# The last 128 query columns of a head in one tile: a rope with half-tile products and a rotation of three twin matmuls

## The chip, the cores and the metric

The kernel runs on one core of a Trainium2 chip. The metric is the device time of one execution in microseconds (us). Three runs of the kernel before took 2216.96, 2220.8 and 2221.03 us, a median of 2220.8 us. The profile is of one further execution.

The engines are named as in the profile: PE (TensorE) multiplies matrices into PSUM, the accumulator memory; PEld is its weight load; DVE (VectorE) and ACT (ScalarE) work elementwise from PSUM or SBUF, the on-chip memory; POOL (GpSimd) works on SBUF; SP issues transfers.

## The reference

The reference is a two-layer block on x of shape (4, 512, 512) in float32. Layer 0 is a top-k sparse adjacency and a ternary feed-forward. Layer 1 is a cross attention with 16 heads and rotary embedding, and a second ternary feed-forward. The change lies in the query side of the layer-1 attention:

```
q_hk  = (hidden_q @ Wq.T).reshape(B, S, 16, 128)
q_big = einsum('bshk,hkq->bshq', q_hk, w_kc_q)        # 384 columns per head
q_big = q_big * cos + rotate_half(q_big) * sin
q_r   = einsum('bshq,hqr->bhsr', q_big, W_qr)         # 64 columns per head
scores = einsum('bhsr,bhlr->bhsl', q_r, k_r)
```

`rotate_half` pairs column i with column i + 192 (the first half gets the second with a minus sign). So each of the 384 columns has one rotation partner, 192 away.

## The kernel before, in words

Tensors stand transposed: query columns lie on partitions and the 512 positions of one batch along the free dimension. 128 partitions hold 128 of the 384 columns. The code names four chunks (`_query_chunks`): a is columns 0-127, a1 is 192-319 (the partners of a), c is 128-191 and c1 is 320-383 (the partners of c). c and c1 have 64 columns each.

Heads are taken in pairs, an even one e and an odd one o; 4 batches times 8 pairs make 32 pairs. `Pair.head(i)` (line 677) computes q_hk of head i. `Pair.rope(i)` (lines 685-710) makes the columns and rotates them:

- `rope(0)` takes a and a1 of head e, `rope(1)` takes a and a1 of head o: two full 128 x 128 matmuls each (line 693), one for a and one for a1.
- `rope(2)` takes the rest of both heads. Its first tile holds c of e on partitions 0-63 and c of o on 64-127, the second holds c1 in the same way. Each tile comes from two matmuls with 64 output columns each, called twins here (`halves`, lines 661-665).

In every rope a tile and its partner tile have the same partitions. So each rotated tile takes two products on DVE over all 128 partitions, ro = tile x cos (line 707) and rs = partner x sin (line 708), and one sum on POOL (line 709).

`Pair.rotated` (lines 712-731) sums q_r of both heads in one PSUM tile pr, with e in partitions 0-63 and o in 64-127. For a and for a1 it issues one twin pair each (e and o side by side). For the tiles of `rope(2)`, which mix e and o along the contraction, it uses two full matmuls (line 726) with a block-diagonal weight: 64 x 64 of e, 64 x 64 of o, zeros elsewhere. ACT then copies pr to SBUF as qr (line 731).

`attention` walks over the 32 pairs. While the current pair does its scores (lines 744 and 747), softmax (752-758), transposes (766), values (774) and output (786), the next pair's `head` and `rope` are mixed in: `rope(2)` in the fourth of four steps, `rotated` after the values. The first pair's head, ropes and rotation stand ahead of the loop.

A generator of background work runs beside it, metered by a table of costs: for batches 1 to 3 the layer-0 adjacency (`adjacency`, whose top-k search alternates a MAX8 at line 403 with a MATCH_REPLACE8 at line 405, 20 rounds for each of four tiles) and the layer-0 feed-forward (`feed0`), later the weights and rows of the second feed-forward (`feed1`). The framework that builds the kernel fixes one order of instructions per engine from the program order and its own estimate of when inputs are ready. So each engine works through a list, and a change of one part shifts background instructions elsewhere in the lists.

PSUM tiles of attention come from a pool of four buffers (`mm_ps`), which pb, pss, pc, pr and po share. The weights of a pair (`query_weights`) are loaded on SP's queue one pair ahead; wr holds the W_qr rows of both heads.

Of the kernel before, what the change touches and what calls it, by code (L numbers as in the profile page):

```python
# [9 lines left out]
F32 = mybir.dt.float32  # L10
BF = mybir.dt.bfloat16
AF = mybir.ActivationFunctionType
ALU = mybir.AluOpType
AX = mybir.AxisListType

P = 128
B, S, D = 4, 512, 512
# [5 lines left out]
NH = 16  # L23
# [10 lines left out]
def flamingo_kernel(  # L34
# [9 lines left out]
    nc = tc.nc  # L44

    const = ctx.enter_context(tc.tile_pool(name="const", bufs=1))
# [5 lines left out]
    hp = ctx.enter_context(tc.tile_pool(name="heads", bufs=2))  # L52
# [5 lines left out]
    def mm_ps(name):  # L58
        return ps.tile([P, 512], F32, tag="mm", name=name)
# [57 lines left out]
    wqk = const.tile([P, 2, DC], F32, tag="wqk", name="wqk")  # L117
    nc.scalar.dma_start(wqk[:, 0, :], wq0T)
    nc.scalar.dma_start(wqk[:, 1, :], wk0T)
    cos_q = const.tile([P, 4, S], F32, tag="cosq", name="cos_q")  # L120
    sin_q = const.tile([P, 4, S], F32, tag="sinq", name="sin_q")

    gx_raw = const.tile([P, 5], F32, tag="graw", name="gx_raw")
    nc.scalar.dma_start(gx_raw[:, 0:2], g_x.partition_broadcast(P))
# [513 lines left out]
    def query_weights(b, g):  # L638

        u = f"{b}_{g}"  # L640
        wqs = []
        for i in range(2):
            wq = hp.tile([P, NC, P], F32, tag="wq", name=f"wq_{u}_{i}")
            nc.sync.dma_start(wq, wqh[2 * g + i])
            wqs.append(wq)
        wc = hp.tile([P, 6 * P], F32, tag="wc", name=f"wc_{u}", bufs=1)
        nc.sync.dma_start(wc, wkcq[g])
        wr = hp.tile([P, 4 * P], F32, tag="wr", name=f"wr_{u}", bufs=1)
        nc.sync.dma_start(wr, wqr[g])
        return wqs, wc, wr  # L650

# [9 lines left out]
    def halves(o, lhs, rhs, **flags):  # L661

        nc.tensor.matmul(o[64:, :], lhs[1], rhs[1], skip_group_check=True, **flags)  # L663
        with tc.high_priority():
            nc.tensor.matmul(o[:64, :], lhs[0], rhs[0], skip_group_check=True, **flags)

    class Pair:
# [17 lines left out]
        def rope(self, i):  # L685


            both = []
            for o in range(2):
                pb = mm_ps(f"pb_{self.u}_{i}_{o}")  # L690
                if i < 2:
                    at = (2 * i + o) * P
                    nc.tensor.matmul(  # L693
                        pb, self.wc[:, at : at + P], self.qhs[i], start=True, stop=True
                    )
                else:
                    at = (4 + o) * P
                    halves(
                        pb, (self.wc[:, at : at + 64], self.wc[:, at + 64 : at + P]), self.qhs,
                        start=True, stop=True,  # L700
                    )
                both.append(pb)
            for o in range(2):
                t = 2 * (i // 2) + o
                ro = wp.tile([P, S], F32, tag="ro", name=f"ro_{self.u}_{i}_{o}", bufs=7)
                rs = wp.tile([P, S], F32, tag="rs", name=f"rs_{self.u}_{i}_{o}", bufs=3)
                nc.vector.tensor_tensor(ro, both[o], cos_q[:, t, :], ALU.mult)  # L707
                nc.vector.tensor_tensor(rs, both[1 - o], sin_q[:, t, :], ALU.mult)  # L708
                nc.gpsimd.tensor_tensor(ro, ro, rs, ALU.add)  # L709
                self.ros.append(ro)  # L710

        def rotated(self):

            wr, ros, u = self.wr, self.ros, self.u
            self.kr = wp.tile([P, S], F32, tag="kr", name=f"kr_{u}", bufs=1)
            nc.sync.dma_start(self.kr, kr_d[self.b, self.g])
            pr = mm_ps(f"pr_{u}")
            for o in range(2):
                halves(
                    pr,  # L720
                    (wr[:, 64 * o : 64 * o + 64], wr[:, P + 64 * o : P + 64 * o + 64]),
                    (ros[o], ros[2 + o]),
                    start=(o == 0), stop=False,
                )
            for o in range(2):
                nc.tensor.matmul(  # L726
                    pr, wr[:, (2 + o) * P : (3 + o) * P], ros[4 + o],
                    start=False, stop=(o == 1), skip_group_check=True,
                )
            self.qr = wp.tile([P, S], F32, tag="qr", name=f"qr_{u}", bufs=1)  # L730
            nc.scalar.copy(self.qr, pr)
            self.pT = [
                wp.tile([P, NT, S], F32, tag="pT", name=f"pT_{u}_{i}") for i in range(2)
            ]
# [58 lines left out]
    def begin(b, g):  # L793
        p = Pair(b, g)
        p.wqs, p.wc, p.wr = query_weights(b, g)
        return p
# [100 lines left out]
    for _ in attention(first):  # L897
        done += 1
        while job < len(jobs):
            gen, cost, until = jobs[job]  # L900
            start = jobs[job - 1][2] if job else 0
# [23 lines left out]
def _hadamard(n):  # L925
    import numpy as np

    h = np.ones((1, 1), np.float32)
    while h.shape[0] < n:
        h = np.block([[h, h], [h, -h]])  # L930
    return np.ascontiguousarray(h, dtype=np.float32)


def _rope(length, dim):
    import numpy as np

    inv = np.float32(1.0) / np.power(
        np.float32(10000.0), np.arange(0, dim, 2, dtype=np.float32) / np.float32(dim)
    )
    f = np.arange(length, dtype=np.float32)[:, None] * inv.astype(np.float32)[None, :]  # L940
    return (
        np.repeat(np.sin(f), 2, axis=-1).astype(np.float32),
        np.repeat(np.cos(f), 2, axis=-1).astype(np.float32),
    )


def _constants():
    import numpy as np

    sin, cos = _rope(S, DQ)  # L950
    half = DQ // 2
    sign = np.where(np.arange(DQ) < half, -1.0, 1.0).astype(np.float32)
    sin = sin * sign
    a, a1, c, c1 = _query_chunks()
    order = np.concatenate([a, a1, c, c, c1, c1])
    q = lambda t: np.ascontiguousarray(t.T[order].reshape(4, P, S).transpose(1, 0, 2))
    cosq, sinq = q(cos), q(sin)
    sin, cos = _rope(S, DC)
    sin = sin * np.where(np.arange(DC) < DC // 2, -1.0, 1.0).astype(np.float32)
    k = lambda t: np.ascontiguousarray(t.reshape(NT, P, DC).transpose(1, 0, 2))  # L960
    return {"had": _hadamard(P), "cosq": cosq, "sinq": sinq, "cosk": k(cos), "sink": k(sin)}


def _query_chunks():

    import numpy as np

    half = DQ // 2
    a, c = np.arange(P), np.arange(P, half)
    return a, a + half, c, c + half  # L970


def _pair_columns(w):

    import numpy as np

    a, a1, c, c1 = _query_chunks()
    e, o = w[0::2], w[1::2]
    return np.concatenate(
        [e[:, :, a], e[:, :, a1], o[:, :, a], o[:, :, a1],  # L980
         e[:, :, c], o[:, :, c], e[:, :, c1], o[:, :, c1]], axis=2
    )


def _pair_rows(w):


    import numpy as np

    a, a1, c, c1 = _query_chunks()  # L990
    e, o = w[0::2], w[1::2]
    z = np.zeros((NH // 2, 64, 64), w.dtype)
    block = lambda r: np.concatenate(
        [np.concatenate([e[:, r], z], axis=2), np.concatenate([z, o[:, r]], axis=2)], axis=1
    )
    return np.concatenate([e[:, a], e[:, a1], o[:, a], o[:, a1], block(c), block(c1)], axis=2)


_OUT = ((B, S, D), "float32")
# [46 lines left out]
```

## Time and profile before

| what | value |
|---|---|
| median of 3 runs | 2220.8 us |
| the profiled execution, its own time | 2219.97 us |
| its span, first to last instruction | 2218.2 us |
| mean granted PE clock | 0.932 |
| PE / DVE / ACT / POOL busy | 1932.9 / 1582.2 / 1225.4 / 350.8 us |
| matmul records, DVE instructions | 7402, 3124 |
| line 726 (block-diagonal matmuls of q_r) | 128 records, 63.8 us |
| lines 663 and 665 in pb (twins of `rope(2)`) | 128 records each, 71.0 us each |
| lines 707 and 708 (rope products on DVE) | 192 each, 130.9 and 131.1 us |
| line 709 (rope sums on POOL) | 192, 256.6 us |

How to read it: a float32 matmul leaves two records. Ends of matmuls are modelled and overlap the next start, so the distance from start to start is the time that a matmul takes of PE. The group lines give, after the bar, busy us, mean ns of one instruction, and the idle time of the engine just before them with what ended it. All engines work at once: idle time counts only on the engine that sets the pace.

### The profile page before, as it was taken

To read this page: it belongs to the slowest core of one execution; us is meant where nothing else is said; L and a number is where in the kernel's file an instruction comes from. 1 tells how busy PE (TensorE), PEld (TensorE's weight loads), DVE (VectorE), ACT (ScalarE), POOL (GpSimd) and SP (SyncE) were. 2 spreads that over 40 slices of the span, in tenths; PEclk is the share of its full clock that TensorE was granted. 3 is DMA by queue.
4 is the path that set the end of the run, shared out by engine and by line. 5 is a ranking of instruction groups with operands and counts; after the bars stand their busy time and mean duration, and the time that the engine had idled before them with its cause. 6 is when DMAs were issued, how large, how long until landed. Compare 5 with 4: busy or idle time off the path is not lost. (4 is left out here: it accounts for less than half of the span.)

```text
span 2218.2 us, 21879 instructions
## 1 busy us (share of the span) xinstructions
PE 1932.9 (87%) x7402; PEld 913.9 (41%) x7402; DVE 1582.2 (71%) x3124; ACT 1225.4 (55%) x1997; POOL 350.8 (16%) x332
## 2 busy tenths in 40 slices
PE   1359789999989989899989888999979999999978
PEld 0125434344444334445443334444434444444433
DVE  7977699976675999665569997566635645756665
ACT  6826444344655543456455543555699565557534
POOL 3032021122110111211111112201211210111000
PEclk6579899999999999899999998999989999999889
DMA  7442011110010211110102111011457101111000
GB/s 275 154 156 94 34 43 38 48 41 27 31 36 24 77 44 36 36 41 24 36 27 83 41 48 36 25 36 32 151 204 244 50 28 53 57 36 34 14 15 20
DMA packets 62176, 140.30 MB, mean 63 GB/s; under 512 B 7152, under 2 KB 10608, under 8 KB 58736
## 3 DMA queue, kind: packets, MB, share of 16 engines
q1 hardware_dynamic: 56592, 122.44, 17.0%
q0 software_dynamic: 4320, 14.16, 1.7%
q10 hardware_dynamic: 1152, 2.30, 0.3%
q8 instruction: 59, 0.97, 0.2%
q14 instruction: 53, 0.43, 0.1%
HBM read 118.95 MB, written 19.92 MB: 63 GB/s over the span
## 5 line engine op out<-in xcount | busy, mean ns | idle before, releaser
L709 POOL TENSOR_TENSOR ro<-ro,rs 128x512 f32<-128x512 f32 x192 | 256.6, 1341 | 1464.0 <-DVE rs L708 1330.7
L755 ACT ACTIVATE pp<-pss,nm 128x512 f32<-128x512 f32 x256 | 174.7, 685 | 247.8 <-DVE nm L752 246.7
L774 PE MATMUL pc<-pT,kv 128*128 128x512 f32 x512 | 259.7, 644 | 8.7 <-ACT pT L767 8.6
L677 PE MATMUL pqh<-hT,wq 128*128 128x512 f32 x512 | 240.2, 608 | 0.7 <-ACT hT L635 0.7
L786 PE MATMUL po<-om,cxo 128*128 128x512 f32 x512 | 229.9, 593 | 0.0
L752 DVE TENSOR_REDUCE nm<-pss 128x1 f32<-128x512 f32 x256 | 169.5, 682 | 65.1 <-PE pss L747 63.8
L403 DVE MAX8 m<-work 128x8 f32<-128x512 f32 x304 | 210.5, 692 | 5.4
L766 PE MATMUL ppt<-ident,pp 128*128 128x128 f32 x1024 | 160.4, 294 | 47.6 <-ACT pp L758 35.5
L405 DVE MATCH_REPLACE8 work<-m,work 128x512 f32<-128x512 f32 x288 | 195.1, 677 | 0.0
L758 ACT ACTIVATE pp<-pp,rsm 128x512 f32<-128x512 f32 x256 | 178.8, 721 | 27.8 <-DVE rsm L757 25.6
L791 DVE SCALAR_TENSOR_TENSOR x<-po,gt,x 128x512 f32<-128x512 f32 x128 | 95.7, 748 | 135.1 <-PE po L786 134.9
L767 ACT COPY pT<-ppt 128x512 f32<-128x512 f32 x256 | 142.7, 588 | 85.8 <-PE ppt L766 84.7
L766 PEld LDWEIGHTS ppt<-ident,pp 128*128 128x128 f32 x1024 | 126.9, 151 | 132.8 <-ACT pp L758 54.7
L707 DVE TENSOR_TENSOR ro<-pb,cos_q 128x512 f32<-128x512 f32 x192 | 130.9, 682 | 34.8 <-PE pb L693 33.9
L744 PE MATMUL pss<-kr,qr 64*128 64x512 f32 x256 | 145.5, 649 | 8.3 <-ACT pp L755 7.7
L747 PE MATMUL pss<-kr,qr 64*128 64x512 f32 x256 | 146.3, 652 | 1.8 <-DVE ro L707 1.3
L677 PEld LDWEIGHTS pqh<-hT,wq 128*128 128x128 f32 x512 | 93.0, 191 | 127.7 <-issue 93.1
L774 PEld LDWEIGHTS pc<-pT,kv 128*128 128x128 f32 x512 | 99.0, 207 | 103.6 <-issue 87.0
L786 PEld LDWEIGHTS po<-om,cxo 128*128 128x128 f32 x512 | 95.8, 190 | 110.0 <-issue 108.1
L693 PE MATMUL pb<-qh,wc 128*128 128x512 f32 x256 | 123.4, 601 | 15.6 <-DVE ro L707 14.9
L708 DVE TENSOR_TENSOR rs<-pb,sin_q 128x512 f32<-128x512 f32 x192 | 131.1, 683 | 7.7 <-PE pb L693 3.5
L779 ACT COPY cxo<-pc 128x512 f32<-128x512 f32 x64 | 37.4, 585 | 120.8 <-PE pc L774 120.7
(256 smaller groups left out, 3285.6 us busy)
## 6 DMA issues: line engine op xcount, KB each, us to landing
wq<-in_wqh SPq DMA_DIRECT2D x64, 256.0 KB, 2.6
om<-omd SPq DMA_DIRECT2D x64, 256.0 KB, 2.7
wc<-in_wkcq SPq DMA_DIRECT2D x32, 384.0 KB, 3.0
wr<-in_wqr SPq DMA_DIRECT2D x32, 256.0 KB, 2.6
krd<-krs POOLq DMA_DIRECT2D x32, 256.0 KB, 2.3
kr<-krd SPq DMA_DIRECT2D x32, 256.0 KB, 2.6
sa_w1v<-in_gvT SPq DMA_DIRECT2D x8, 1024.0 KB, 5.0
sb_w1v<-in_gvT SPq DMA_DIRECT2D x8, 1024.0 KB, 6.5
```

The lines of the kernel that those rows point to most:

```text
L403: nc.vector.max(m8, cur)
L405: nc.vector.match_replace(work, m8, cur, GONE)
L677: nc.tensor.matmul(pq, self.wqs[i][:, c, :], hT[self.b][:, c, :], start=(c == 0), stop=(c == NC - 1),)
L709: nc.gpsimd.tensor_tensor(ro, ro, rs, ALU.add)
L744: nc.tensor.matmul(*args, start=True, stop=True)
L747: nc.tensor.matmul(*args, start=True, stop=True)
L752: nc.vector.tensor_reduce(nm, pss[i], AX.X, ALU.max, negate=True)
L755: nc.scalar.activation(pp, pss[i], AF.Exp, bias=nm, accum_out=sm)
L758: nc.scalar.activation(pp, pp, AF.Copy, scale=rs)
L766: nc.tensor.transpose(pt[:, l, :], pp[:, l * P : (l + 1) * P], ident)
L774: nc.tensor.matmul(pc, kv[self.b][:, l, :], self.pT[i][:, l, :], start=(l == 0), stop=(l == NT - 1),)
L786: nc.tensor.matmul(po, self.cxo[i][:, j * P : (j + 1) * P], self.oms[i], start=(i == 0), stop=(i == 1),)
```

## The change

The 64 + 64 remaining columns of one head now share a tile: `rope(2)` puts c and c1 of head e into its first tile, and c and c1 of head o into its second. The rotation partner of a column then lies in the same tile, 64 partitions away.

- The two tiles come from one full 128 x 128 matmul each, like those of the other ropes. `halves` is no longer used there.
- The cos and sin tables have three tiles instead of four; the third serves both heads.
- For the tiles of `rope(2)` the product with sin is done in two halves: partitions 64-127 of the tile go to partitions 0-63 of rs, and 0-63 to 64-127. The products with cos and the sums stay whole.
- `rotated` issues three twin pairs, since now every rotated tile belongs to one head. The block-diagonal weight is gone, and wr shrinks from four to three blocks of 128 columns.
- On the host, weights and tables are laid out to match.

```diff
-    cos_q = const.tile([P, 4, S], F32, tag="cosq", name="cos_q")
-    sin_q = const.tile([P, 4, S], F32, tag="sinq", name="sin_q")
+    cos_q = const.tile([P, 3, S], F32, tag="cosq", name="cos_q")
+    sin_q = const.tile([P, 3, S], F32, tag="sinq", name="sin_q")
...
-        wr = hp.tile([P, 4 * P], F32, tag="wr", name=f"wr_{u}", bufs=1)
+        wr = hp.tile([P, 3 * P], F32, tag="wr", name=f"wr_{u}", bufs=1)
...
-                if i < 2:
-                    at = (2 * i + o) * P
-                    nc.tensor.matmul(
-                        pb, self.wc[:, at : at + P], self.qhs[i], start=True, stop=True
-                    )
-                else:
-                    at = (4 + o) * P
-                    halves(
-                        pb, (self.wc[:, at : at + 64], self.wc[:, at + 64 : at + P]), self.qhs,
-                        start=True, stop=True,
-                    )
+                at = (2 * i + o) * P
+                nc.tensor.matmul(
+                    pb, self.wc[:, at : at + P], self.qhs[i if i < 2 else o], start=True, stop=True
+                )
                 both.append(pb)
             for o in range(2):
-                t = 2 * (i // 2) + o
+                t = o if i < 2 else 2
...
                 nc.vector.tensor_tensor(ro, both[o], cos_q[:, t, :], ALU.mult)
-                nc.vector.tensor_tensor(rs, both[1 - o], sin_q[:, t, :], ALU.mult)
+                if i < 2:
+                    nc.vector.tensor_tensor(rs, both[1 - o], sin_q[:, t, :], ALU.mult)
+                else:
+                    for to, fro in ((slice(0, 64), slice(64, P)), (slice(64, P), slice(0, 64))):
+                        nc.vector.tensor_tensor(rs[to, :], both[o][fro, :], sin_q[to, t, :], ALU.mult)
                 nc.gpsimd.tensor_tensor(ro, ro, rs, ALU.add)
...
-            for o in range(2):
+            for o in range(3):
+                at = 2 * o * 64
                 halves(
-                    pr,
-                    (wr[:, 64 * o : 64 * o + 64], wr[:, P + 64 * o : P + 64 * o + 64]),
-                    (ros[o], ros[2 + o]),
-                    start=(o == 0), stop=False,
-                )
-            for o in range(2):
-                nc.tensor.matmul(
-                    pr, wr[:, (2 + o) * P : (3 + o) * P], ros[4 + o],
-                    start=False, stop=(o == 1), skip_group_check=True,
+                    pr, (wr[:, at : at + 64], wr[:, at + 64 : at + P]),
+                    (ros[o], ros[2 + o]) if o < 2 else (ros[4], ros[5]),
+                    start=(o == 0), stop=(o == 2),
                 )
```

More of the change, by code (lines that the diff above doesn't have):

```diff
@@ L953, in _constants @@
     sin = sin * sign
-    a, a1, c, c1 = _query_chunks()
-    order = np.concatenate([a, a1, c, c, c1, c1])
-    q = lambda t: np.ascontiguousarray(t.T[order].reshape(4, P, S).transpose(1, 0, 2))
+    order = np.concatenate(_query_chunks())
+    q = lambda t: np.ascontiguousarray(t.T[order].reshape(3, P, S).transpose(1, 0, 2))
     cosq, sinq = q(cos), q(sin)
@@ L979, in _pair_columns @@
     return np.concatenate(
-        [e[:, :, a], e[:, :, a1], o[:, :, a], o[:, :, a1],
-         e[:, :, c], o[:, :, c], e[:, :, c1], o[:, :, c1]], axis=2
+        [w_[:, :, r] for w_, r in ((e, a), (e, a1), (o, a), (o, a1), (e, c), (e, c1), (o, c), (o, c1))],
+        axis=2,
     )
@@ L990, in _pair_rows @@
     a, a1, c, c1 = _query_chunks()
[L991 to L996, printed above, removed]
+    last = np.concatenate([c, c1])
+    return np.concatenate([w_[:, r] for r in (a, a1, last) for w_ in (w[0::2], w[1::2])], axis=2)
 _OUT = ((B, S, D), "float32")
```

## The prediction

> **What bounds the kernel now.** I read the page's busy line first, then the busy table in stretches that I cut at the copies of q_r (line 731, one per pair of heads), then the groups by shape, then the timeline of one pair on PE and on DVE.
>
> ```profile
> PE 1932.9 (87%) x7402; PEld 913.9 (41%) x7402; DVE 1582.2 (71%) x3124; ACT 1225.4 (55%) x1997; POOL 350.8 (16%) x332
> ```
>
> This is an average over stages with different limits. The stretches are more useful (start:end, length, then busy us and instructions of PE, PEld, DVE, ACT, POOL; granted clock; DMA):
>
> ```profile
> 0.00:308.70 308.70, 179.27 (x730) 95.01 (x730) 241.31 (x486) 176.16 (x217) 67.03 (x98) 0.78 0.37 131
> 308.70:432.30 123.60, 112.77 (x361) 49.07 (x362) 120.77 (x261) 62.61 (x121) 22.81 (x18) 0.99 0.15 44
> 432.30:748.30 316.00, 293.03 (x1173) 141.83 (x1172) 222.13 (x409) 162.54 (x290) 52.19 (x46) 0.96 0.11 33
> 748.30:889.60 141.30, 128.09 (x379) 54.96 (x378) 133.27 (x298) 64.16 (x122) 22.84 (x18) 0.94 0.18 57
> 889.60:1203.30 313.70, 291.67 (x1171) 143.45 (x1170) 205.71 (x368) 167.02 (x293) 54.39 (x46) 0.96 0.11 34
> 1203.30:1343.60 140.30, 127.01 (x380) 54.37 (x379) 134.97 (x302) 64.04 (x121) 22.82 (x18) 0.95 0.19 58
> 1343.60:1598.90 255.30, 239.24 (x987) 120.41 (x987) 158.61 (x265) 139.01 (x242) 46.79 (x40) 0.95 0.15 49
> 1598.90:1663.30 64.40, 52.39 (x175) 24.69 (x174) 25.48 (x55) 58.71 (x71) 7.62 (x6) 0.87 0.63 223
> 1663.30:2052.20 388.90, 371.75 (x1416) 165.14 (x1415) 234.54 (x469) 253.77 (x400) 54.35 (x42) 0.99 0.22 71
> ```
>
> Of the 31 pair iterations between 308.7 and 2052.2, nine (308.7-432.3, 748.3-889.6, 1203.3-1343.6) run beside a top-k search. There DVE is busy 98%, 94% and 96% and idles only 2.8 + 8.0 + 5.3 = 16.1 us in all. One (1598.9) sits at ACT 91%. The other 21 have PE at 93-96% and DVE at 60-70%. So PE sets the pace of 21 pairs and DVE that of nine, nearly. The rest (0-308.7 and after 2052.2) holds one rope and one rotation only.
>
> Now one rotation on PE, lines 663, 665 and 726:
>
> ```profile
> 1294.80 0.64 PE L663 MATMUL pr<-ro,wr 128*64 128x512 f32 x1
> 1294.81 0.64 PE L665 MATMUL pr<-ro,wr 128*64 128x512 f32 x1
> 1295.28 0.59 PE L663 MATMUL pr<-ro,wr 128*64 128x512 f32 x1
> 1296.14 0.59 PE L663 MATMUL pr<-ro,wr 128*64 128x512 f32 x1
> 1296.67 1.98 PE L726 MATMUL pr<-ro,wr 128*128 128x512 f32 x4
> 1298.49 1.45 PE L786 MATMUL po<-om,cxo 128*128 128x512 f32 x3
> ```
>
> A float32 matmul leaves two records, 0.43 us from start to start. Twins start 0.01 us apart, so a twin pair takes 0.86 us like one full matmul. All 32 rotations have this pattern or the same with background work between.
>
> ```profile
> L709 POOL TENSOR_TENSOR ro<-ro,rs 128x512 f32<-128x512 f32 x192 | 256.6, 1341 | 1464.0 <-DVE rs L708 1330.7 <-DVE rsm L757 65.8 <-DVE s_hf L182 49.6
> L708 DVE TENSOR_TENSOR rs<-pb,sin_q 128x512 f32<-128x512 f32 x192 | 131.1, 683 | 7.7 <-PE pb L693 3.5 <-PE pb L665 3.0 <-PE ppt L766 1.2
> ...
> L726 PE MATMUL pr<-ro,wr 128*128 128x512 f32 x128 | 63.8, 614 | 0.3 <-POOL ro L709 0.2
> ```
>
> A DVE product reads 683 ns, but the next independent one follows sooner; one that depends on the last follows later:
>
> ```profile
> 1285.71 0.70 DVE L403 MAX8 m<-work 128x8 f32<-128x512 f32 x1
> 1286.31 0.69 DVE L708 TENSOR_TENSOR rs<-pb,sin_q 128x512 f32<-128x512 f32 x1
> ...
> 1287.69 0.69 DVE L403 MAX8 m<-work 128x8 f32<-128x512 f32 x1
> 1288.42 0.09 DVE L405 MATCH_VALUE_LOAD work<-m,work 128x8 f32 x1
> ```
>
> Independent step 0.60 us, dependent step 0.73: a wait for the end costs 0.13.
>
> **What the Trainium skill says.** "TensorE: Matmul & The Clock Gate", Part 3: matmuls on different column groups run concurrently; the trace agrees (0.01 us). "TensorEngine Tiling (Array Packing)", Key Properties: changing the tiling mode drains the array; the trace shows 0.52-0.53 us instead of 0.43 on each side of a twin block (1296.14 to 1296.67), plus 0.05-0.10 on the second step. "VectorE: DVE Perf Modes", § Why `tensor_reduce` can't reduce along partition axis: DVE streams along the free dimension, so half the partitions should not halve the time; no run here shows a 64-partition DVE product. Same page, § Two Vector instructions with no wait between them: an instruction that starts in another quadrant than the last access to that memory is held until all earlier ones have finished; before has no such case. The dependent step (0.13 more) is my nearest row for it.
>
> **The change, part by part**, in microseconds per pair.
>
> 1. Last rotation on PE. Two full matmuls (4 records, 1.72) become one twin pair (0.86): -0.86. One mode change in, one out, as before. PE is dense here: in the 31 pairs pc, pr and po (or background matmuls between them) follow each other without a pause. The new pair needs both last sums at once; POOL kept line 726 waiting 0.2 us in the whole run, and 16 records of pc (6.9 us) lie between rope and rotation, so its later sums stay covered.
>
> 2. Rope 2 on PE. Two twin pairs (1.72) become two full matmuls (1.72), without the drain at the end (0.09) and the late weights (0.05-0.10): -0.2. Both together: -1.06.
>
> 3. Rope 2 on DVE. Four full products become two full and four half ones. Unheld, a half product takes 0.60: +2 x 0.595 = 1.19. Each half product starts its PSUM, its sine or its output in another quadrant than its forerunner, and the instruction behind it changes back: about six holds, 6 x 0.13 = 0.78. Together +1.97, which I take. Bounds: below 1.19 nothing speaks for; above, half products that take twice 0.68.
>
> 4. POOL: the same 192 sums, 84% idle; it waits for a later DVE. PSUM: the second pb is freed after six DVE products instead of three, the first after three instead of four; the next users of these two buffers are pr and po, some 7 us later. No cost.
>
> 5. DMA: wr 192 instead of 256 KB, landed in 2.6 us some 35 us ahead of use: nothing. The two tables are 768 KB instead of 1 MB each, on ACT's queue at 6 and 21 us, beside the first weight loads. In the built order the first weight's sum moves ahead of one search instruction. From 0 to -2; I take 0, since DVE's search fills that stretch. No step passes another on SP's or POOL's queue.
>
> 6. First rope and rotation (299-309): six POOL sums back to back (300.1 to 307.5) set the end, and DVE's last product ends at 306.0, 0.3 us before the last sum starts. With +1.97 there: +1.6.
>
> 7. Order. In the built order of the changed kernel the nine DVE pairs hold 175 search rounds instead of 178 (three more fall into the fourth pair, which has idle DVE); a round is two instructions, 1.3 us: -3.9 of DVE time. In PE-bound pairs the order moves attention matmuls ahead of background transposes that would come late (at 1064 five pc matmuls stand before ptq_hf, seven in the new order), so the later DVE is largely covered there.
>
> Sum. 21 PE-bound pairs: -1.06 x 21 = -22.3. I keep 85%, -18.9: where background waits for DVE right behind rope 2, as q_f at 1063.9, half a microsecond before its transpose, part of the gain turns into a wait. Nine DVE pairs: +1.97 x 9 = 17.7, less 3.9 moved, less 40% of 16.1 idle (6.5): +7.3; PE's gain there goes into waiting for DVE. The ACT pair: 0. Start: +1.6. Total -10.0: the profiled span of 2218.2 becomes 2208.2 and its execution of 2220.0 becomes 2210.0; the median of the runs is 0.8 above that execution, so 2210 to 2211; I say 2210.
>
> **Rivals.**
>
> A. Whole gain: holds are cheap and DVE's extra falls into slack, since background, not attention, is pushed back. Then 21 x 1.06 + 9 x 0.86 = 30, less 1.6 at the start: 2192. For it: the new order puts two or three search rounds fewer between rope 2 and the residual adds. Against: DVE idles only 2 to 6% there.
>
> B. The gain becomes waits: PE reaches its next wait sooner and DVE answers later. Keeping 40% of PE's gain (-9), +9 in the DVE pairs and +1.6: 2222. For it: ACT waited for DVE's maxima (246.7 us) and reciprocals (25.6 us) in all, and PE stands behind ACT there. Against: PE stands still little in the 21 pairs.
>
> C. Slower: one half product, shifted between partition halves, costs far more than a full one. With a step s, DVE gains 4s - 1.19 per pair. At s = 1.36 that is 4.25: nine pairs +38.2 - 3.9 - 6.5 = +27.8, the start +3.9, less 18.9: 2234. It decides from 9(4s - 1.19) - 10.4 + (4s - 1.19) - 0.3 = 18.9, s = 1.04 us. For it: no row shows such an instruction. Against: per-lane streaming.
>
> **How the numbers follow.** Forecast 0.45 (own range 2199 to 2217), A 0.18, B 0.20, C 0.17. The range 2190 to 2230 leaves out the far ends of A and C. A change under 0.2% (4.4 us) can't be told from none here. Faster: nearly all of the forecast, A, a little of B: 0.63. Same: most of B: 0.17. Slower: C and a rest of B: 0.20.
>
> **What would show it.** PE records fall from 7402 to 7274, DVE instructions rise to 3188. From the start of the last pc to that of the first po a rotation shrinks from 4.21 to 3.25 us (0.52 in, 2.20 to the last twins, 0.53 out), with 0.10 more on the next step. The half products read about 0.68 with steps of 0.7-0.8. The nine pairs lengthen by about 0.8 each, the 21 shorten by 0.9. The forecast is wrong if half products step above 1.0 us, if the twins don't overlap, or if the PE-bound pairs don't shorten.

## The result and the profile after

The changed kernel takes 2211.36 us, median of 6 runs (2208.83 to 2212.74). Six runs of the kernel before on the same chip gave 2219.21 us (2216.7 to 2221.03). The ratio is 0.9965 with a 95% interval of 0.9952 to 0.9978: 0.35% faster, 7.9 us. The profiled execution took 2211.89 us with a span of 2210.1 us, 8.1 us less than the span before.

The busy line of the page of after:

```profile
PE 1905.4 (86%) x7274; PEld 904.6 (41%) x7274; DVE 1628.4 (74%) x3188; ACT 1217.0 (55%) x1990; POOL 350.8 (16%) x332
```

PE has 128 records fewer and is busy 27.5 us less, DVE has 64 instructions and 46.2 us more. Both counts are the forecast ones, and the net is a small difference of two larger effects. Where each of them went is read from the stretches of after, cut again at the copies of q_r (line 723 now), with the columns of before:

```profile
309.90:436.00 126.10, 113.93 (x349) 49.55 (x349) 121.12 (x258) 63.24 (x120) 22.83 (x18) 0.95 0.14 42
436.00:747.40 311.40, 285.69 (x1153) 139.50 (x1154) 230.62 (x420) 162.66 (x290) 51.77 (x46) 0.97 0.11 32
747.40:889.70 142.30, 128.73 (x367) 54.60 (x368) 137.02 (x304) 63.34 (x122) 22.83 (x18) 0.94 0.18 55
889.70:1200.50 310.80, 287.63 (x1151) 142.65 (x1152) 219.36 (x390) 163.76 (x290) 54.68 (x46) 0.96 0.12 33
1200.50:1340.70 140.20, 126.22 (x367) 53.94 (x368) 134.16 (x298) 64.33 (x122) 22.83 (x18) 0.94 0.19 56
1340.70:1595.00 254.30, 234.54 (x971) 119.31 (x971) 166.74 (x279) 138.90 (x241) 47.09 (x40) 0.96 0.16 46
1595.00:1664.50 69.50, 53.21 (x172) 25.48 (x173) 27.78 (x57) 60.92 (x73) 7.62 (x6) 0.83 0.65 225
1664.50:2045.90 381.40, 363.93 (x1386) 163.23 (x1384) 240.57 (x474) 248.96 (x398) 54.46 (x42) 0.99 0.22 69
```

Compare lengths with the same rows of before. The nine pairs beside a search (rows 1, 3 and 5) went from 405.2 to 408.6 us, +3.4. DVE still fills them: it idles 5.0 + 5.3 + 6.0 = 16.3 us there, as before. The 21 pairs that PE paces (rows 2, 4, 6 and 8) went from 1273.9 to 1257.9 by these rounded cuts, -15.8 by the unrounded ones. The pair with the weight loads (row 7) grew by 5.0. The start (0 to 309.9) grew by 1.2, and the tail after the last pair shrank by 1.8.

The rotation itself, from the PE timeline of after (start, duration, instruction):

```profile
1289.68 1.02 PE L766 MATMUL pc<-pT,kv 128*128 128x512 f32 x2
1290.63 0.64 PE L663 MATMUL pr<-ro,wr 128*64 128x512 f32 x1
1290.64 0.64 PE L665 MATMUL pr<-ro,wr 128*64 128x512 f32 x1
...
1292.83 0.59 PE L663 MATMUL pr<-ro,wr 128*64 128x512 f32 x1
1293.36 2.84 PE L778 MATMUL po<-om,cxo 128*128 128x512 f32 x6
```

The last pc record starts at 1290.11 (the second of the first line). It is 0.52 us to the first twins, 2.20 from there to the last twins (1292.83) and 0.53 to po: 3.25 us, where the old pattern takes 4.21. In 22 rotations of each kernel nothing stands between pc, pr and po, and all of them show these two numbers.

The new products, from the DVE timeline and from the groups of after:

```profile
1053.46 0.69 DVE L700 TENSOR_TENSOR ro<-pb,cos_q 128x512 f32<-128x512 f32 x1
1054.17 1.39 DVE L705 TENSOR_TENSOR rs<-pb,sin_q 64x512 f32<-64x512 f32 x2
1055.59 0.69 DVE L700 TENSOR_TENSOR ro<-pb,cos_q 128x512 f32<-128x512 f32 x1
```

```profile
L705 DVE TENSOR_TENSOR rs<-pb,sin_q 64x512 f32<-64x512 f32 x128 | 88.1, 688 | 3.1
L702 DVE TENSOR_TENSOR rs<-pb,sin_q 128x512 f32<-128x512 f32 x128 | 87.0, 679 | 5.2 <-PE pb L692 5.2
```

A product over 64 partitions reads 688 ns, one over 128 partitions 679 ns: half the partitions save nothing. The halves step by 0.71 us. Over the whole trace, a half product follows a half product by 0.706 us (28 cases without idle time), while an independent full product steps by 0.598. The difference is 0.11 us. It could be the hold of the forecast, or half products could simply step later; e_group below separates the two and finds 0.09 us for the hold.

### The profile page after: what moved, and what is told of

Read it like the earlier page. It is cut to its first block, busy times and chain, and to the rows that moved or that the text cites. A ratio compares the mean times of both kernels' runs of the same rounds, so it can differ in the third digit from the quotient of the medians.

```text
span 2210.1 us, 21671 instructions
## 1 busy us (share of the span) xinstructions
PE 1905.4 (86%) x7274; PEld 904.6 (41%) x7274; DVE 1628.4 (74%) x3188; ACT 1217.0 (55%) x1990; POOL 350.8 (16%) x332
## 4 chain that ended last, share of the span: by engine, by line
PE 55%; DVE 31%; ACT 9%; issue 3%; DMA 2%; POOL 0%; ACTq 0%; SPq 0%; DVEq 0%; POOLq 0%
PE pc L766 11%; PE po L778 8%; DVE work L405 6%; DVE m L403 6%; PE pqh L677 5%; PE pr L663 4%; DVE nm L744 3%; PE pzh_f L502 3%; PE pb L692 2%; PE ppt L758 2%; PE pss L736 2%; PE pu_g L291 2%; DVE rs L702 2%; DVE ro L700 2%; PE pd_g L363 2%
## 5 line engine op out<-in xcount | busy, mean ns | idle before, releaser
L692 PE MATMUL pb<-qh,wc 128*128 128x512 f32 x384 | 193.1, 618 | 17.1 <-DVE ro L700 14.9
L750 ACT ACTIVATE pp<-pp,rsm 128x512 f32<-128x512 f32 x256 | 178.8, 720 | 23.9 <-DVE rsm L749 21.3
L692 PEld LDWEIGHTS pb<-qh,wc 128*128 128x128 f32 x384 | 67.6, 192 | 106.8 <-issue 40.2
```

The costliest lines, as they stand in the source:

```text
L692: nc.tensor.matmul(pb, self.wc[:, at : at + P], self.qhs[i if i < 2 else o], start=True, stop=True)
L750: nc.scalar.activation(pp, pp, AF.Copy, scale=rs)
```

## Experiments

The theory: PE's shorter rotation is worth most of 1.06 us in each of the 21 pairs that PE paces, and DVE's two additional instructions give part of it back, in the nine pairs beside a search above all. The rivals of the prediction stand against it: A (DVE's part costs nothing), B (the PE part mostly turns into waits), C (a half product is dear). The runs first take the two parts of the change apart, then look for a cheaper place for the swap of partition halves.

This table gives, for the profiled span of each kernel, the difference of every group of stretches to before, in us. It is worked out from the same cuts as above (D: the nine pairs beside a search; P: the 21 pairs that PE paces; W: the pair with the weight loads). The last three columns are of P alone: the mean granted clock of PE (1 is full speed), the idle time of PE in us, and its busy time in us multiplied by that clock:

```
                    start      D      P      W   tail   total   clock   idle  busy x clock
before                 0      0      0      0      0       0  0.9692   78.2  1158.8
after                +1.2   +3.4  -15.8   +5.0   -1.8    -8.1  0.9729   86.1  1140.1
e_full               +1.0   -2.2  -20.5   +3.4   -3.9   -22.3  0.9728   82.5  1139.0
e_before_halves      +3.7  +10.7   -4.3   +0.3   -3.8    +6.5  0.9771   82.4  1160.1
e_before_shifted     +1.6  +14.1   -3.4   -1.1   -4.1    +7.1  0.9785   83.6  1161.3
e_drop               -1.1   -1.6  -19.6   +1.6   -3.8   -24.5  0.9714   84.2  1136.6
e_act_pool           +6.8  +12.0  +27.1   -0.9   -4.0   +41.0  0.9580  113.4  1137.6
e_act_dve            +4.0   +9.3  +17.3   -0.9   -3.8   +26.0  0.9617  108.7  1137.1
e_abs_after          +3.1   +2.9  -14.1  +10.9   -2.2    +0.7  0.9716   87.9  1138.6
e_swap_dma           +7.0   +2.1  -27.2   +4.5   -2.6   -16.2  0.9767   80.3  1139.2
e_group              +1.6   +2.9  -17.7   +4.5   -2.3   -11.0  0.9715   83.3  1139.5
e_swap_first         +1.1   +1.4  -28.4   +4.3   -2.9   -24.5  0.9781   80.7  1139.2
```

The tail is 1.8 to 4.1 us shorter than in the profile of before in every kernel, also in the two that save nothing on PE. The granted clock in the tail was 0.886 in before and 0.903 to 0.933 in the others. So the shorter tail is not credited to the change.

The clock has to be read with P, too. Busy time multiplied by clock is 1158.8 to 1161.3 us in the three kernels that have all matmuls of before, and 1137.1 to 1140.1 us in the eight with the new ropes and rotation. PE's work in P thus fell by about 20 us in all of these. The column P is spread much wider, by idle time and by the clock: at 0.978, the clock of e_swap_first, the 1195.6 us that PE is busy in P of before would be 11 us shorter. What set the clock of each profile is not shown. It differs between executions of one kernel as well: among the executions of e_before_halves with a mean clock above 0.95, the four at 0.959 took 2216.45 to 2218.03 us and those at 0.953 and 0.952 took 2229.66 and 2229.77 us. One profile per kernel therefore fixes P and the tail only to several us.

**PE's part alone: e_full.** The change with one whole sine product per tile, without the swap.

```diff
-    for to, fro in ((slice(0, 64), slice(64, P)), (slice(64, P), slice(0, 64))):
-        nc.vector.tensor_tensor(rs[to, :], both[o][fro, :], sin_q[to, t, :], ALU.mult)
+    nc.vector.tensor_tensor(rs, both[o], sin_q[:, t, :], ALU.mult)
```

> The changed kernel, but the sine product of the last rope is one whole product of the tile with itself instead of two half products of swapped partitions: the rotation of these 128 columns is left out, so the PE part of the change stands alone. Theory (PE sets 21 pairs, DVE nine, and DVE's two more products with their holds are paid in those nine): about 1.8 us less DVE per pair, the nine pairs fall from 415 us to about 403, the start loses its extra 1.2 us, total 2198 (2193 to 2204). Rival (DVE's extra is covered by idle time, and the small gain is what the instruction order left): no change from 2211 by more than 3 us.

Measured: 2197.72 us (4 runs, 2196.95 to 2200.82), ratio to before 0.9901 [0.9886, 0.9915], as expected. In the source only the two DVE instructions per pair are different from after, and with the order of instructions that follows from them they cost 2211.36 - 2197.72 = 13.6 us. In the profiles the groups P, D, W and tail differ by 4.7, 5.6, 1.6 and 2.1; the start does not (0.2), where 1.2 had been expected. So PE's part was worth about 23 us in the runs (before took 2220.91 us beside them), and DVE's part takes more than half of it back. Rival A (2192) comes nearest to this kernel, not to the changed one.

**DVE's part alone: e_before_halves and e_before_shifted.** The kernel before with its last sine product cut in two, without and with the crossing of halves.

```diff
-    nc.vector.tensor_tensor(rs, both[1 - o], sin_q[:, t, :], ALU.mult)
+    if i < 2:
+        nc.vector.tensor_tensor(rs, both[1 - o], sin_q[:, t, :], ALU.mult)
+    else:
+        for to in (slice(0, 64), slice(64, P)):
+            nc.vector.tensor_tensor(rs[to, :], both[1 - o][to, :], sin_q[to, t, :], ALU.mult)
```

That is e_before_halves; e_before_shifted has this loop in its place:

```diff
+        for to, fro in ((slice(0, 64), slice(64, P)), (slice(64, P), slice(0, 64))):
+            nc.vector.tensor_tensor(rs[to, :], both[1 - o][fro, :], sin_q[to, t, :], ALU.mult)
```

> The kernel before with its last sine product in two half products, not swapped: the DVE part of the change alone, with the count of instructions but no exchange of halves. Theory: +1.19 us for two instructions and about +0.4 for four holds per pair; nine pairs +14 less some 10 that idle time and moved search rounds take, start +1.3, the rest little: 2225 (2221 to 2230). Rival (covered): 2219, within 2 us.

> As the run with two half products in the kernel before, but each half product reads the other half of its tile, as in the change (the rotation is then not the reference's). Theory: the exchange itself is free, only one or two more holds of 0.11 us per pair: 2226, within 3 us of the unswapped run. Rival (the exchange costs time of its own): a half product reads over 0.8 us and the run lies above 2235.

Measured: e_before_halves 2223.99 us (22 runs, 2216.45 to 2231.38), ratio 1.0011 [1.0000, 1.0021]; e_before_shifted 2225.38 (11 runs, 2222.02 to 2231.11), ratio 1.0022 [1.0013, 1.0030]. The groups of the half products, first without the crossing, then with it:

```profile
L712 DVE TENSOR_TENSOR rs<-pb,sin_q 64x512 f32<-64x512 f32 x128 | 87.4, 682 | 3.8 <-PE pb L665 2.3
```

```profile
L712 DVE TENSOR_TENSOR rs<-pb,sin_q 64x512 f32<-64x512 f32 x128 | 88.1, 689 | 4.8 <-PE pb L665 1.7
```

The crossing adds 7 ns to an instruction and 0.02 us to the step from half to half (0.688 and 0.706 us, 28 cases each). It also adds a hold in front of the first half: the step from the cosine product to it is 0.605 us without the crossing (19 of 20 cases) and 0.707 with it. Most of the cost is the second instruction, not the swap. D is where it is paid: +10.7 and +14.1 us. P and the tail are shorter by about 8 us together though nothing was saved on PE; PE's work in P (1160.1 and 1161.3) is that of before, and the clock was higher in both groups. So the shares worked out from P below are no finer than that. This is rival C's question settled: the half product steps by 0.71 us, below the 1.04 from which C decides.

**PE's saving without the rest of the change: e_drop.** The kernel before with one block-diagonal matmul per pair left out.

```diff
-            for o in range(2):
-                nc.tensor.matmul(
-                    pr, wr[:, (2 + o) * P : (3 + o) * P], ros[4 + o],
-                    start=False, stop=(o == 1), skip_group_check=True,
-                )
+            nc.tensor.matmul(
+                pr, wr[:, 3 * P : 4 * P], ros[5], start=False, stop=True, skip_group_check=True,
+            )
```

> The kernel before with one of its two block-diagonal matmuls left out (the tile of c is not added to q_r): the 0.86 us of PE per pair alone, with DVE, POOL and the layout as before. Theory: 21 PE-bound pairs give most of it, 21 x 0.86 x 0.85 = 15, the nine DVE pairs little, the pair at the second weight load takes some back: 2204 (2199 to 2209). Rival (the gain turns into waits for DVE and ACT everywhere): 2213 or above.

Measured: 2195.44 us (6 runs, 2185.01 to 2202.13), ratio 0.9887 [0.9868, 0.9906]. This is faster than expected. The 21 pairs lost 19.6 us where 21 x 0.86 = 18.1 were taken from PE; 2.7 of the 19.6 go with the clock, so about 17 would be left at the clock of before. As closely as P can tell, PE's time is kept nearly whole there. The theory of the PE-paced pairs stands, and rival B (40% kept) is excluded for PE's part by itself.

**Why after keeps less.** In after P shrank by 15.8 us against 21 x 1.06 = 22.3, in e_full by 20.5. These two had the same clock in P (0.973), so they can be compared: P is 4.7 us longer in after, and PE idles 3.6 us more in it. The waits of PE at the softmax transposes and the values, in after:

```profile
PE ppt L758 <- ACT pp L750: 43.6, 23, 5.0
...
PE ppt L758 <- ACT pT L759: 12.8, 14, 3.2
PE pc L766 <- ACT pT L759: 12.3, 22, 1.8
```

The columns are us in all, times, and the longest. The same three waits in before:

```profile
PE ppt L766 <- ACT pp L758: 35.5, 19, 4.7
...
PE ppt L766 <- ACT pT L767: 9.9, 11, 2.2
...
PE pc L774 <- ACT pT L767: 8.6, 17, 0.7
```

They sum to 68.7 us in after and 54.0 before, and to 58.0 in e_full. In the 21 pairs alone PE idles 86.1 us in after and 78.2 before, 7.9 more, of which these three waits make 5.2. So part of the gain does turn into waits, as rival B has it, but a small part. How much of it is B's mechanism stays open: PE idles 4.1 and 5.4 us more in P also in the two kernels that save nothing on PE. That ACT comes later because DVE does is argued, not shown: ACT's own waits for DVE's reciprocals were 21.3 us in after and 25.6 before.

**ACT as the place of the swap: e_act_pool and e_act_dve.** ACT copies the swapped halves; POOL, or DVE in one whole instruction, then does the sine product.

```diff
-        nc.vector.tensor_tensor(rs[to, :], both[o][fro, :], sin_q[to, t, :], ALU.mult)
+        nc.scalar.copy(rs[to, :], both[o][fro, :])
+    nc.gpsimd.tensor_tensor(rs, rs, sin_q[:, t, :], ALU.mult)     # e_act_pool
+    nc.vector.tensor_tensor(rs, rs, sin_q[:, t, :], ALU.mult)     # e_act_dve, in its place
```

> The changed kernel, but ACT copies the two swapped halves of the tile into rs and POOL does the whole sine product there: per pair DVE loses four products of the change (two fewer than the kernel before), ACT gains four half copies (about 2.3 us), POOL two products (2.7 us). Theory (DVE's share of the change is what it paid in the nine search pairs): those pairs fall below the kernel before, PE gain as in the run with whole products: 2192 (2185 to 2202). Rival (ACT's copies come late for the softmax scaling that PE waits for): 2205 or above.

> As the last one, but DVE does the whole sine product in place after ACT's swapped copies: DVE has as many products as the kernel before and no half ones, ACT gains four half copies per pair. Theory: near the run with whole products, 2199 (2193 to 2206). Rival (ACT's copies delay the softmax): 2208 or above.

Measured: e_act_pool 2260.82 us (4 runs, 2254.42 to 2263.33), ratio 1.0181 [1.0163, 1.0199]; e_act_dve 2246.81 (4 runs, 2245.72 to 2249.98), ratio 1.0127 [1.0110, 1.0144]. The theory missed both by 48 to 69 us. P, not D, shows the loss: +27.1 and +17.3. The groups of e_act_pool, PE's transposes and then the new copies:

```profile
L759 PE MATMUL ppt<-ident,pp 128*128 128x128 f32 x1024 | 159.4, 294 | 91.0 <-ACT pT L760 47.1 <-ACT pp L751 42.1 <-ACT hT L635 1.6
...
L705 ACT COPY rs<-pb 64x512 f32<-64x512 f32 x128 | 74.2, 580 | 8.8 <-DVE ro L700 6.5
```

and the transposes in after:

```profile
L758 PE MATMUL ppt<-ident,pp 128*128 128x128 f32 x1024 | 159.6, 293 | 58.2 <-ACT pp L750 43.6 <-ACT pT L759 12.8 <-ACT hT L635 1.5
```

ACT is busy 57% of e_act_pool as an average. But four copies of 0.58 us per pair, 2.3 us, stand in its list ahead of the copies of transposes (pT) that PE waits for, and that wait grew from 12.8 to 47.1 us. In 18 of its 20 cases, 43.4 us, two to four of the new copies ran just before. The growth is 34 of the 49 us by which this span is longer than that of after; in P the clock was lower as well, 0.958 against 0.973. PE's matmuls waited 6.0 us in all for POOL at the rotation, so POOL's additional products cost PE little there. DVE issues 64 instructions fewer than before the change, and D still grew by 12.0 us.

**ACT's load in the weight pair: e_abs_after.** W grew by 5.0 us in after. A first explanation was that ACT, 88% busy there, had become the bound. Here one kind of ACT work of that stretch, the absolute sums of the weights, is put on DVE.

```diff
-                junk = bp.tile([P, FF], BF, tag="q", name=f"ja_{name}{i}") if hold else t
-                nc.scalar.activation(junk, t, AF.Abs, accum_out=acc[:, i : i + 1])
+                if hold:
+                    junk = bp.tile([P, FF], BF, tag="q", name=f"ja_{name}{i}")
+                    nc.scalar.activation(junk, t, AF.Abs, accum_out=acc[:, i : i + 1])
+                else:
+                    nc.vector.tensor_reduce(
+                        acc[:, i : i + 1], t, AX.X, ALU.add, apply_absolute_value=True
+                    )
```

> The changed kernel with the absolute sums of the second feed-forward's weights (twelve passes of 1.9 us) on DVE instead of ACT. Theory for the lost time at that load (the pair at 1595 became 5 us longer although DVE is idle 60% there: PE comes sooner to a wait for ACT's weight passes): the pair at the load falls from 69.4 us to about 60, total 2203 (2198 to 2209). Rival (the loss there is an accident of the order, not ACT's load): the pair stays within 2 us, total 2209 or above.

Measured: 2217.16 us (14 runs, 2212.47 to 2223.21), ratio 0.9993 [0.9983, 1.0004]. W became 10.9 us longer than before, not shorter. ACT then idled 24.2 us in W instead of 8.5 in after, so its load alone does not set the length. But the run is no clean test of that load: PE waited 11.0 us for the first weight's sum, which now came from DVE, instead of 5.0. What the traces show of W is this. After holds 19 of ACT's 2-us weight passes where before holds 18, and the next pair holds 10 instead of 12, so one pass of 2 us only moved across the cut. PE's waits in W grew from 12.0 to 16.3 us: 1.5 at the first weight's sum, the rest mostly at the copies of transposes. And the clock in W was 0.83 instead of 0.87. Why ACT's list came out in that order at that place stays open.

**Order within rope 2: e_group.** Both lower halves first, then both upper halves, behind both cosine products.

```diff
-                    for to, fro in ((slice(0, 64), slice(64, P)), (slice(64, P), slice(0, 64))):
-                        nc.vector.tensor_tensor(rs[to, :], both[o][fro, :], sin_q[to, t, :], ALU.mult)
-                nc.gpsimd.tensor_tensor(ro, ro, rs, ALU.add)
...
+            if i == 2:
+                for to, fro in ((slice(0, 64), slice(64, P)), (slice(64, P), slice(0, 64))):
+                    for o in range(2):
+                        nc.vector.tensor_tensor(
+                            pair[o][1][to, :], both[o][fro, :], sin_q[to, 2, :], ALU.mult
+                        )
+                for ro, rs in pair:
+                    nc.gpsimd.tensor_tensor(ro, ro, rs, ALU.add)
```

> The changed kernel with its four half products issued behind both cosine products and grouped by the half they read, so that the quadrant changes less often where nothing stands between them. Theory (about 0.11 us per hold): 3 holds fewer per pair at most, 0.3 us of DVE in nine pairs: 2209 (2205 to 2214), hardly to be told from 2211. Rival (the order of the last sums and the later release of the first buffer matter more): 2215 or above.

Measured: 2208.04 us (5 runs, 2206.9 to 2209.23), ratio 0.9956 [0.9944, 0.9969]. The interval overlaps that of after (0.9952 to 0.9978), so a gain from fewer changes between halves is not shown; with a hold of 0.1 us it could only be small. The trace of this run shows the hold by itself, between instructions of one shape: where a half product follows one of the same half without idle time it steps by 0.61 us (26 cases), and where it follows one of the other half by 0.70 (16 cases).

**A DMA queue as the place of the swap: e_swap_dma and e_swap_first.** One whole sine product with a table stored with its halves exchanged, then two transfers on SP's queue that exchange the halves of the result. POOL adds the exchanged tile.

```diff
-                    for to, fro in ((slice(0, 64), slice(64, P)), (slice(64, P), slice(0, 64))):
-                        nc.vector.tensor_tensor(rs[to, :], both[o][fro, :], sin_q[to, t, :], ALU.mult)
+                    nc.vector.tensor_tensor(rs, both[o], sin_q[:, t, :], ALU.mult)
+                    rw = wp.tile([P, S], F32, tag="rw", name=f"rw_{self.u}_{o}", bufs=2)
+                    nc.sync.dma_start(rw[0:64, :], rs[64:P, :])
+                    nc.sync.dma_start(rw[64:P, :], rs[0:64, :])
+                    rs = rw
...
+    sinq[:, 2] = np.roll(sinq[:, 2], 64, axis=0)
```

> The changed kernel with one whole sine product per tile (the third sine tile is stored with its halves exchanged to match) and the exchange of the product's halves done by two SBUF-to-SBUF transfers of 128 KB on SP's queue into a further tile, which POOL then adds. DVE has as many products as the kernel before, PE those of the change. Theory (the change's cost is the two further DVE products and their holds): near the run with whole products, 2199 (2193 to 2206), since about 7 us of value matmuls lie between rope and rotation, and a load lands in 2.6 us. Rival (the transfers, or SP's queue that waits for them, come late for the rotation or for the next weights): 2208 or above, and PE waits at the rotation for POOL.

Measured: 2199.95 us (5 runs, 2197.3 to 2203.99), ratio 0.9921 [0.9907, 0.9934]. The issue line of this page and POOL's wait for the transfers:

```profile
rw<-rs SPq DMA_DIRECT2D x128, 128.0 KB, 2.3
```

```profile
POOL ro L709 <- DMA rw<-rs: 199.2, 37, 16.6
```

A transfer lands 2.3 us after its issue (2.2 to 5.8). POOL waits for it, but PE hardly waits for POOL. The only waits of PE's matmuls at the rotation are these:

```profile
PE pr L663 <- POOL ro L709: 6.2, 3, 4.9
```

All three are in the first pair, where nothing lies between rope and rotation. The start is 7.0 us longer. From the first matmul of that pair's ropes to its copy of q_r it takes 16.1 us, before 11.8; the other 2.6 us are lost ahead of these ropes. So the last version, e_swap_first, keeps the half products for the first pair alone. They read the sine of the other half, since the table stays exchanged:

```diff
-                else:
+                elif alone[0]:
                     for to, fro in ((slice(0, 64), slice(64, P)), (slice(64, P), slice(0, 64))):
-                        nc.vector.tensor_tensor(rs[to, :], both[o][fro, :], sin_q[to, t, :], ALU.mult)
+                        nc.vector.tensor_tensor(rs[to, :], both[o][fro, :], sin_q[fro, t, :], ALU.mult)
+                else:
+                    nc.vector.tensor_tensor(rs, both[o], sin_q[:, t, :], ALU.mult)
...
```

> As the run that exchanges the halves by transfers, but the first pair, whose rope and rotation stand ahead of the loop with nothing beside them, takes the change's half products. Theory: the 7.0 us that the start lost with the transfers shrink to about 1.2, the rest stays: 2195 (2190 to 2201). Rival (the start's loss has another cause, such as the order of the first loads): 2199 or above.

Measured: 2197.41 us (4 runs, 2195.45 to 2200.21), ratio 0.9900 [0.9883, 0.9916]. The busy line of its page:

```profile
PE 1898.1 (87%) x7274; PEld 906.0 (41%) x7274; DVE 1578.8 (72%) x3126; ACT 1221.5 (56%) x1994; POOL 351.3 (16%) x332
```

DVE is back at 1578.8 us, PE keeps its 128 records less, and the start is +1.1 instead of +7.0. The first pair's ropes and rotation take 13.8 us, so 2.3 of the 5.9 won at the start are due to the half products; the rest is won ahead of these ropes, by what is not shown. This version does all of the rotation, and its interval agrees with that of e_full, which leaves the swap out: the swap costs nothing that these runs can tell. It is 14 us faster than the changed kernel and 1.0% faster than before. P alone shrank by 28.4 us, more than the 22.3 that PE could save there; some 11 of them go with the clock of 0.978 (before 0.969). Of the 14 us to after, about 6 go with the clock in the same way (0.978 against 0.973), and whether this version itself brings the higher clock is not shown.

## Why the prediction was right

The forecast of 2210 us with faster as the likeliest sign holds: 2211.36 us. Its sum was -10.0; the profile shows -8.1. The mechanism was right: PE's shorter rotation pays in the pairs that PE paces, and DVE's additional instructions take part of it back. That the total came so near is in part luck, since errors of 2 to 5 us in single terms cancel. Term by term:

| term | forecast | profile |
|---|---|---|
| 21 PE-paced pairs | -18.9 | -15.8 |
| nine pairs beside a search | +7.3 | +3.4 |
| the pair with weight loads | 0 | +5.0 |
| start | +1.6 | +1.2 |
| tail | 0 | -1.8 |

**Steps 1 and 2, PE.** Held in every part: 7274 records, 0.52 in, 2.20, 0.53 out. The size -1.06 per pair is near what was found: PE's work in P fell by 18.7 to 21.7 us, 0.9 to 1.0 per pair at full clock. "I keep 85%" was probably too much: after shows 71% (15.8 of 22.3), but 4.5 us of it go with the clock of 0.973 instead of 0.969, and at the clock of before about half would be left. The same working gives 72% for e_full and 94% for e_drop; one profile of each does not fix the shares. The reason given, a wait behind rope 2, is partly borne out: PE idles 7.9 us more in the 21 pairs, and 3.6 of these are not there without DVE's two instructions. The waits stand mostly at the softmax transposes and the values (5.2 us), with 1.0 us at q_f, where the step had them. "Its later sums stay covered" holds nearly: PE's matmuls waited 4.2 us for POOL at the rotation, 1.6 before.

**Steps 3 and 7, DVE.** The kind was right, all three sizes were off. (a) +1.97 per pair: the nine pairs show about 1.5. (b) Three rounds moved, -3.9: by the instructions that start in the nine pairs, MAX8 went from 180 to 174 and MATCH_REPLACE8 from 171 to 165, six rounds, and two instructions that end a search (0.74 us each) left as well. A round is dearer than 1.3 us when nothing stands in it: 131 such rounds of before take 1.52 from start to start. So up to 10.6 us left, and with the 3.4 by which the pairs grew this makes 14.0, or 1.6 a pair for (a). In e_before_shifted the pairs grew by 14.1, lost some 2.4 of search and idled 3.6 more on DVE, which leaves 12.9, or 1.4 a pair. Six holds of 0.1 with 1.19 for the instructions would be 1.8; what covers the rest is not settled. (c) 40% of the idle 16.1 us filled, -6.5: none of it was; DVE idles 16.3 us. The errors cancel: 17.7 - 3.9 - 6.5 = 7.3 was forecast, 14.0 - 10.6 = 3.4 came.

"VectorE: DVE Perf Modes" of the Trainium skill, section on reducing along the partition axis, was the ground for expecting that 64 partitions take as long as 128: 688 against 679 ns agrees. Its section on two Vector instructions with no wait between them gives the hold without a price; e_group shows a step of 0.70 us with it and 0.61 without, where the forecast had 0.13 for it.

**Step 6, the start.** +1.2 for +1.6. The reason is right, though the sum is near by luck: from the first matmul of the first ropes to the first copy of q_r after takes 14.0 us, before 11.8 and e_full, without DVE's two instructions, 11.8 as well. That is +2.2, and in after this part began 1.0 us earlier.

**The pair with weight loads.** "The ACT pair: 0" is the step that failed. It was taken as bound by ACT and therefore unmoved. It grew by 5.0 us: 2 us of ACT's work came in across its edge, PE's waits grew by 4.3 us, and the clock was 0.83 instead of 0.87. Moving ACT's sums to DVE did not mend it. e_drop, with PE's saving and no more DVE work, has +1.6 there, and the two kernels with DVE's part alone have +0.3 and -1.1. So neither part by itself makes it. All kernels with the new ropes and rotation and no work on ACT have +3.4 to +5.0 there (leaving out e_abs_after), so it goes with the two together, perhaps by the order of instructions; by which step is not shown.

**The tail.** It was left out of the sum and gave -1.8; the clock there was 0.915 instead of 0.886.

**Step 4 and step 5, POOL, PSUM and transfers.** Nothing contradicts them: POOL is at 350.8 us, as before, and nothing waits for a table.

**The rivals.** A (2192) comes near e_full (2197.7), in which DVE's extra is taken out. B's waits exist, but PE's additional idle time in the 21 pairs is 7.9 us and not 60% of 22.3. C is excluded by a step of 0.71 us.

## What to carry to other kernels

On DVE a product over half the partitions costs as much as one over all: count instructions, not elements, and look at the stretches in which DVE is full before adding one. A swap of partition halves is best given to an engine or queue that nobody in that stage waits for: here two 2.3-us transfers under several microseconds of other work cost nothing that the runs can tell, while 0.58-us copies on an ACT that is 55% busy on average cost 35 to 50 us, for the most part because PE stands behind ACT at the transposes. Before a few us in one group of a profile are put down to a change, compare the granted clock in that group. Where the same step also runs once without cover, keep the form with the shorter latency there.

## What the runs showed of the hardware that was not expected

The whole sine product of e_act_dve has both inputs in SBUF. On average it is slower than the one with an input in PSUM. The two groups of that kernel:

```profile
L702 DVE TENSOR_TENSOR rs<-pb,sin_q 128x512 f32<-128x512 f32 x128 | 86.9, 679 | 5.4 <-PE pb L692 5.4
...
L706 DVE TENSOR_TENSOR rs<-rs,sin_q 128x512 f32<-128x512 f32 x64 | 57.9, 906 | 25.5 <-ACT rs L705 25.3
```

The mean of 906 ns hides two kinds. The 35 products during which POOL runs nothing take 0.67 to 0.69 us, so neither the place of the inputs nor writing over the own input is slow. The other 29 run beside an instruction of POOL and take 0.67 to 1.76 us. Two of these, each with the sums of POOL beside it (start, duration, instruction; the last line holds two sums):

```profile
1208.38 1.06 DVE L706 TENSOR_TENSOR rs<-rs,sin_q 128x512 f32<-128x512 f32 x1 [0.24 <-ACT rs L705]
1207.62 1.27 POOL L707 TENSOR_TENSOR ro<-ro,rs 128x512 f32<-128x512 f32 x1 [4.94 <-DVE rs L706]
...
1074.18 0.68 DVE L706 TENSOR_TENSOR rs<-rs,sin_q 128x512 f32<-128x512 f32 x1
1074.28 3.91 POOL L707 TENSOR_TENSOR ro<-ro,rs 128x512 f32<-128x512 f32 x2 [8.62 <-DVE m_hf L180]
```

In the first, POOL's sum ends at 1208.89 and the product 0.55 us later. So it is with all 26 products that start while an instruction of POOL is already running: they end 0.55 to 0.57 us after it. In the second, the product starts first and takes its usual 0.68 us, and POOL's first sum takes 1.70 us instead of 1.27; there are three such cases (1.56 to 1.70 us). In this kernel a DVE product from SBUF and a POOL sum thus do not proceed together: the one that starts later waits for the other. Over the 29 products this makes about 14 us of DVE's time. The rope products that read PSUM take 677 and 678 ns on average beside POOL and 678 and 680 without it.

Reading and writing different partition halves in one DVE instruction costs 7 ns (689 against 682). A transfer of 128 KB from SBUF to SBUF lands in 2.3 us, about as the transfers of 256 KB on the page of e_swap_dma (2.3 to 2.9 us).
